# GroupNorm 2 computed in two halves of the images, and four images' edge products put behind the last spectrum product

## The chip, the core and the metric

The kernel runs on one core of a Trainium2 chip. The metric is the device time of one execution in microseconds (us). Times before the change: 1701.88, 1690.03, 1691.06, 1700.30 and 1711.91 us, median 1700.3 us. One further execution was taken with the hardware profiler; all trace times below are us from the start of its span.

Engines: PE (TensorE, matrix products), ACT (ScalarE), DVE (VectorE), POOL (GpSimd), SP (SyncE, which here only issues DMAs). Each executes its instructions in order, and an instruction that waits for a semaphore holds up all that stand behind it on that engine.

## What is computed

The input is x, 16 images of 64 channels of 128x128 pixels, float32. Two layers follow each other.

```python
# layer 0: a Hartley spectral convolution with 20x20 modes, a Gaussian blur over all 4 axes, a column mask
y = gaussian_smoothing_4d(dht_2d(modes_20x20(dht_2d(x)) mixed by w1))
x = y * mask
# layer 1
residual = x
h = group_norm(x, gn1_w, gn1_b)               # 8 groups
h = afno(h, ...)                              # 32x32 Fourier modes, two small complex layers with GELU
h = h + residual
residual = h
h = group_norm(h, gn2_w, gn2_b)               # GroupNorm 2
feats = gelu(conv1x1(h, fe_w, fe_b))
shared = mean over 2 of gelu(conv1x1(feats, shared_w[s]))
gate_w = top 4 of 16 experts, softmax, from the pixel mean of feats through small dense layers
out = shared + sum_e gate_w[e] * gelu(conv1x1(feats, expert_w[e])) + residual
```

Everything up to the second GroupNorm is linear in a few modes or acts on 32x32 modes, so the kernel stays in mode space until then. GroupNorm 2's mean and variance are also computed in mode space, and its scale and shift are folded into the weights `fsa` (one 64x64 matrix per image) and the bias `fba` of the first 1x1 convolution.

## The kernel before

The work stands in four stages of one program.

1. **Forward transform and mode mixing** (up to L367, some 265 us). The result is `ot`: 400 modes by 16 images x 64 channels.
2. **GroupNorm 1 in mode space** (L433 to L531).
3. **The spectrum loop** (`for b in range(NB)`, L630 to L659), one turn per image. Within a turn PE computes the image's 32x32 complex spectrum in two halves (L640, tiles `psx`, 32 instructions each, in two passes); the first small layer of the image before it (`layer1`, L576, with a GELU on ACT, L580); the second small layer of that image (`layer2`, L588); and `edges(b)` (L562), a product that gives the corrections at the image's borders. `layer2` ends in much work on other engines: an ACT pass with the bias (L591), two squares with accumulation for GroupNorm 2's variance (L605), on DVE a transposition (L595), copies (L599) and products with accumulation (L606), on ACT two negations (L600), and two DMAs of 512 KB that store the tile `bs` to DRAM (`bmd`, L601). `edges` ends in one DVE pass to the tile `eh` (L566) and a DMA of 130 KB to DRAM (`ehd`, L567). In turns 0 to 9 `modes(b)` runs as well (L541, L544); in turns 10 to 13 `modes_out` makes two scaled copies (L551 on ACT, L552 on DVE) and POOL issues 12 DMAs of 100 KB for each (L555). After the loop `layer2(*layer1(*first))` (L660) handles image 15.
   The tiles `xk`, `xr`, `eh`, `o1`, `o2` and `bs` have two buffers each (pool `s_w`, L627): `eh` of image b+2 can be written only when the DMA of image b has read its buffer, and the same holds for `bs`.
   A scheduler orders each engine's instructions in this stage.
4. **The pixel loop** (L975 to L989). Here the order is written out by hand (`PIECES`, L966): pieces of several images are interleaved by due times. Per image: `spectrum` (L700) loads `bm`, one single-buffered tile, in eight DMAs from DRAM (four of `bmd`, L707; four with 80-byte runs, L710) and the edge corrections (L705); `columns` (L712) transforms columns in four quarters on PE (L717), which ACT copies to the tile `u` (L721); `pixels` (L726) transforms rows in eight tiles (L737), which ACT (L748) or DVE (L750, L752) copy to the tiles `h`; `feature` (L798) does the first 1x1 convolution with `fsa` on PE (L808) and a GELU with `fba` on ACT (L812), eight per image; `gate` (L818) chooses the experts and has POOL gather their weights; `group` (L948) runs 48 convolutions per image (PE L898, GELU on ACT L903, weighted sum on DVE L907 or L913). All of this stage's PSUM comes from one pool of four double banks (`ps2`).

GroupNorm 2 is the generator `norm2` (L758). In the program before it is run once, for all 16 images, inside the pixel loop: two of its steps behind each of the first quarters of `columns` of image 0 (L985 to L987). It holds four small products on PE (L769, L775, L783, L794), some 17 short DVE instructions on 16 columns, one DVE pass that writes `fsa` for all images (L790) and one power on POOL (L786). Image 0's first `feature` needs its result.

Of the kernel before, what the change touches and what calls it, by code (L numbers as in the profile page):

```python
# [11 lines left out]
F32 = mybir.dt.float32  # L12
AF = mybir.ActivationFunctionType
ALU = mybir.AluOpType
# [4 lines left out]
NB, C, N = 16, 64, 128  # L19
# [6 lines left out]
EPS = 1e-5  # L26
# [8 lines left out]
WHOLE, SIDES = (slice(0, N),), (slice(0, N // 2), slice(N // 2, N))  # L35
BY_ACT = (0, 2, 4, 6)
CL = C // 2
NSL = 8


# [142 lines left out]
def hartley_afno_moe_kernel(ctx: ExitStack, tc: tile.TileContext, a: dict, out: bass.AP):  # L183
    nc = tc.nc
    P = 128
# [229 lines left out]
    col = lambda i, p=P: vec[0:p, i:i + 1]  # L415


    sq_pool = ExitStack()
    with tc.tile_pool(name="s_o", bufs=1) as so, \
            tc.tile_pool(name="s_p1", bufs=2, space=PSUM) as pp1, \  # L420
# [10 lines left out]
        HB, HG = NB // 2, NB // 2 * 8  # L431

        QB = NB // 4  # L433
        st = sc.tile([P, QB * C], F32, name="st")
# [148 lines left out]
        def layer2(b, o1, xr):  # L583

            ps = pp3.tile([P, 2, 512], F32, name="pso")
            for j, h in ((0, 0), (1, 1), (0, 1), (1, 0)):
                g = slice(j * C, (j + 1) * C)
                nc.tensor.matmul(ps[h * C:(h + 1) * C, j], lhsT=wx2[g, h].rearrange("p r c -> p (r c)"),  # L588
                                 rhs=o1[g, h], start=True, stop=True)
# [5 lines left out]
            nc.vector.transpose(bs[:, :, 0].rearrange("p c m -> p m c"), o2.rearrange("p (m c) -> p m c", c=MD))  # L595
            junkv, o2v, xrv = (v.rearrange("p (m c) -> p m c", c=MD) for v in (junk, o2, xr))
            for h in range(2):
                re, im = (slice(h * C + r * MD, h * C + (r + 1) * MD) for r in range(2))
                nc.vector.tensor_copy(bs[re, :, 1], bs[im, :, 0])  # L599
                nc.scalar.mul(bs[im, :, 1], bs[re, :, 0], -1.0)  # L600
                nc.sync.dma_start(bmd[b, :, h * CL:(h + 1) * CL],  # L601
                                  bs[h * C:(h + 1) * C].rearrange("p c r m -> p c (r m)"))
# [23 lines left out]

        sw = sq_pool.enter_context(tc.tile_pool(name="s_w", bufs=2))  # L627
        junk = sc.tile([P, MD * MD], F32, name="junk")
        first = second = None
        for b in range(NB):  # L630
            xk = sw.tile([P, MD * MD], F32, name="xk")
            xr = sw.tile([P, MD * MD], F32, name="xr")
            for n in range(2):
                cols = slice(n * 512, (n + 1) * 512)
                ps = pp2.tile([P, 512], F32, name="psx")
                for kc in range(4):
                    for h in range(2):
                        for ri in range(2):
                            p0 = h * C + ri * CL
                            nc.tensor.matmul(  # L640
                                ps[p0:p0 + CL], lhsT=ot[:, kc, b * C + h * CL:b * C + (h + 1) * CL],
                                rhs=spec[:, kc, ri * 1024 + n * 512:ri * 1024 + (n + 1) * 512],
                                start=(kc == 0), stop=(kc == 3))
                nc.vector.tensor_scalar(xk[:, cols], ps, gx[:, 0, b:b + 1], None, ALU.mult)
                nc.scalar.copy(xr[:, cols], ps)
                if n == 0:
                    nc.vector.tensor_scalar(xk[:, 0:1], xk[:, 0:1], gx[:, 1, b:b + 1], None, ALU.add)
                    if first:
                        second = layer1(*first)
                elif second:  # L650
                    layer2(*second)
            first = (b, xk, xr)
            edges(b)
            if b == HB:
                bn1s, bn1f, bn2s, bn2f = prepare()
            if b < K // 2:
                modes(b)
            elif b < K // 2 + QB:
                modes_out(b - K // 2)  # L659
        layer2(*layer1(*first))  # L660
        sq_pool.close()

    on_modes.close()


    with s3:
        up_, hpp, fp, gp, selp = (pool(n, q) for n, q in (
            ("u", 1), ("hp", 13), ("feats", 10), ("g", 7), ("selw", 2)))
        stgp = pool("stg", 1)
        ps2 = pool("ps2", 4, space=PSUM)  # L670


# [2 lines left out]
        def few_columns():  # L675
            return ps2.tile([P, 2, 512], F32, name="pe").rearrange("p h n -> p (h n)")[:, 0:2 * NB]
# [49 lines left out]
        def pixels(box, t):  # L726
# [31 lines left out]
        def norm2():  # L758

            w = smp.tile([P, 2, NB], F32, name="n2w")  # L760
            k = smp.tile([P, 2, NB], F32, name="n2k")
            nc.vector.tensor_tensor(w[:, 1], dcs, fold[:, P:P + 1].to_broadcast([P, NB]), ALU.mult)
            nc.vector.scalar_tensor_tensor(k[:, 0], acc[:, :, 2], 2.0, acc[:, :, 3], ALU.mult, ALU.add)
            nc.vector.scalar_tensor_tensor(k[:, 0], k[:, 0], 2.0, one_s[:, 1], ALU.mult, ALU.mult)
            nc.vector.scalar_tensor_tensor(k[:, 1], acc[:, :, 0], 2.0, k[:, 0], ALU.mult, ALU.add)
            nc.vector.scalar_tensor_tensor(w[:, 0], acc[:, :, 1], 0.5, k[:, 1], ALU.mult, ALU.add)
            yield
            z = few_columns()
            nc.tensor.matmul(z, lhsT=fold[:, 0:P], rhs=w.rearrange("p i b -> p (i b)"), start=True, stop=True)  # L769
            mh, vh = k[:, 0], k[:, 1]  # L770
            nc.vector.scalar_tensor_tensor(mh, z[:, NB:], 1.0 / N, base[:, 0], ALU.mult, ALU.add)
            nc.vector.scalar_tensor_tensor(vh, z[:, 0:NB], 1.0 / (N * N), base[:, 1], ALU.mult, ALU.add)
            yield
            z = few_columns()
            nc.tensor.matmul(z[:, 0:NB], lhsT=grp, rhs=mh, start=True, stop=True)  # L775
            m, d = w[:, 0], w[:, 1]
            nc.vector.tensor_copy(m, z[:, 0:NB])
            nc.vector.tensor_tensor(d, mh, m, ALU.subtract)
            nc.vector.tensor_tensor(d, d, d, ALU.mult)
            nc.vector.tensor_tensor(d, d, vh, ALU.add)  # L780
            yield
            z = few_columns()
            nc.tensor.matmul(z[:, 0:NB], lhsT=grp, rhs=d, start=True, stop=True)  # L783
            s, t = k[:, 0], k[:, 1]
            nc.vector.tensor_scalar(s, z[:, 0:NB], EPS, None, ALU.add)
            nc.gpsimd.tensor_tensor(s, s, mhalf[:, 0:1].to_broadcast([P, NB]), ALU.pow)  # L786
            nc.vector.tensor_scalar(s, s, col(V_GN2W), None, ALU.mult)
            nc.vector.tensor_tensor(t, m, s, ALU.mult)
            nc.vector.tensor_scalar(t, t, -1.0, col(V_GN2B), ALU.mult, ALU.add)
            nc.vector.tensor_tensor(fsa, fe2.unsqueeze(1).to_broadcast([P, NB, C]),  # L790
                                    s.unsqueeze(2).to_broadcast([P, NB, C]), ALU.mult)
            yield
            z = few_columns()
            nc.tensor.matmul(z[:, 0:NB], lhsT=few, rhs=t, start=True, stop=True)  # L794
            nc.vector.tensor_scalar(fba, z[:, 0:NB], col(V_FEB), None, ALU.add)
            yield

        def feature(box, t):  # L798
            if t == 0:
# [260 lines left out]
```

## Time and profile before

| | us |
|---|---|
| median of 5 executions (lowest, highest) | 1700.3 (1690.03, 1711.91) |
| the profiled execution, as timed | 1695.38 |
| its span, first to last instruction | 1693.6 |
| last spectrum product (L640) of image 15 ends | 502.4 |
| first quarter of `columns` of image 0 starts (L717) | 513.4 |
| its last quarter ends | 532.9 |
| first `feature` GELU of image 0 starts on ACT (L812) | 538.7 |
| its last one ends | 556.7 |
| pixel loop from then on, per image | 71 to 72 |
| mean granted TensorE clock over the span | 0.969 |

A timeline row gives the start, the duration, the engine, the source line, the operation, the output and input tiles, the shapes, a count where neighbours were merged, and in square brackets how long the engine had been idle before it and what ended that. The queue rows (SPq) give the issue of a DMA, not its landing. The windows view gives, for each stretch, the busy time of each engine, the TensorE clock granted in it as a share of full speed, the mean share of the 16 DMA engines that was busy, and GB/s. float32 products go through PE in two passes, so the counts of PE rows are twice those of the code.

### The profile page before, as it was taken

How to read it: one execution, taken by the hardware profiler on the slowest of the kernel's cores; microseconds unless marked ns; L12 is line 12 of the kernel's file. 1: busy time of each engine (PE TensorE's matmuls, PEld its weight loads, DVE VectorE, ACT ScalarE, POOL GpSimd, SP SyncE). 2: the span in 40 equal slices, each digit the busy share in tenths (PEclk: the TensorE clock that was granted, in tenths of full speed). 3: DMA queues.
4: the chain of work that ended last, by engine and by line, in shares of the span. 5: the costliest groups of instructions: out<-in, count | busy, mean ns of one | idle time of the engine just before them, and what ended most of it. 6: DMA issues, size and time to landing. Idle time of an engine off the chain costs nothing.

```text
span 1693.6 us, 61048 instructions
## 1 busy us (share of the span) xinstructions
PE 1557.7 (92%) x27144; PEld 846.3 (50%) x27144; DVE 1267.9 (75%) x1700; ACT 1272.8 (75%) x1631; POOL 150.3 (9%) x152
## 2 busy tenths in 40 slices
PE   7999958799997999999999999999999999999974
PEld 7988855233326545444444444444445445454420
DVE  0344423456663798988989889998899988999986
ACT  2233334255664898988989899998899988999975
POOL 0000011000131101101010110100101011010120
PEclk9999979899997999999999999999999999999997
DMA  9988964353574234555445555555454555545447
GB/s 385 334 311 305 309 137 122 83 129 85 129 181 108 43 46 83 90 89 92 72 81 81 100 93 74 85 82 99 89 74 85 82 100 89 75 85 81 70 72 113
DMA packets 398861, 205.02 MB, mean 121 GB/s; under 512 B 366842, under 2 KB 371942, under 8 KB 396222
## 3 DMA queue, kind: packets, MB, share of 16 engines
q1 hardware_dynamic: 394134, 193.76, 53.4%
q0 software_dynamic: 4464, 7.35, 1.8%
q8 instruction: 214, 3.51, 0.9%
q14 instruction: 49, 0.40, 0.1%
HBM read 109.86 MB, written 91.20 MB: 119 GB/s over the span
## 4 chain that ended last, share of the span: by engine, by line
PE 70%; issue 9%; DMA 9%; ACT 6%; DVE 4%; SPq 1%; POOL 1%; DVEq 0%; POOLq 0%; ACTq 0%
PE pe L898 31%; PE ps L274 8%; PE pe L717 7%; PE psx L640 6%; PE pe L737 5%; PE pe L808 5%; DMA wl<-exd,ati 5%; ACT g L903 3%; PE ps L235 3%; DMA spec_sb<-in_spec_dram 1%; PE psd L562 1%; PE psd L541 1%; DVE h L907 1%; PE pso L588 1%; PE pso L576 1%
## 5 line engine op out<-in xcount | busy, mean ns | idle before, releaser
L903 ACT ACTIVATE g<-pe,wl 128x1024 f32<-128x1024 f32 x512 | 552.3, 1201 | 49.1 <-PE pe L898 48.5
L898 PE MATMUL pe<-f,wl 64*64 64x512 f32 x4096 | 495.7, 605 | 41.5 <-DMA wl<-exd,ati 41.5
L907 DVE SCALAR_TENSOR_TENSOR h<-g,wt,h 128x1024 f32<-128x1024 f32 x384 | 472.5, 1279 | 33.9 <-ACT g L903 33.1
L907 DVE SCALAR_TENSOR_TENSOR h<-g,h 128x1024 f32<-128x1024 f32 x256 | 300.9, 1216 | 13.1 <-ACT g L903 13.1
L898 PEld LDWEIGHTS pe<-f,wl 64*64 64x64 f32 x4096 | 147.9, 135 | 267.1 <-issue 154.4
L903 ACT ACTIVATE g<-pe,vec_sb 128x1024 f32<-128x1024 f32 x256 | 269.0, 1115 | 11.5 <-PE pe L898 11.4
L898 PE MATMUL pe<-f,shw 64*64 64x512 f32 x2048 | 244.2, 595 | 0.8 <-DVE sco L850 0.4
L274 PE MATMUL ps<-fwd_sb,xt 128*64 128x64 f32 (+1 forms) x3584 | 176.2, 233 | 19.6 <-issue 13.4
L737 PEld LDWEIGHTS pe<-inv_sb,u 64*64 64x64 f32 x8192 | 155.7, 142 | 67.8 <-issue 41.8
L274 PEld LDWEIGHTS ps<-fwd_sb,xt 128*64 128x64 f32 (+1 forms) x3584 | 163.0, 147 | 24.7 <-issue 15.1
L277 ACT COPY t<-ps 128x320 f32<-128x320 f32 x128 | 53.8, 426 | 154.6 <-PE ps L274 154.4
L737 PE MATMUL pe<-inv_sb,u 64*64 64x64 f32 x8192 | 158.6, 227 | 1.9 <-ACT u L721 1.1
L913 DVE SCALAR_TENSOR_TENSOR stg<-g,wt,h 128x1024 f32<-128x1024 f32 x128 | 158.4, 1278 | 1.3 <-DMA bm<-obd 0.7
L812 ACT ACTIVATE f<-pe,fba 128x1024 f32<-128x1024 f32 x128 | 153.6, 1210 | 3.2 <-PE pe L808 3.2
L717 PEld LDWEIGHTS pe<-inv_sb,bm 116*64 116x64 f32 x4096 | 129.3, 142 | 51.9 <-ACT g L903 34.9
L717 PE MATMUL pe<-inv_sb,bm 116*64 116x64 f32 x4096 | 138.3, 228 | 2.1 <-issue 1.3
L808 PE MATMUL pe<-h,fsa 64*64 64x512 f32 x1024 | 132.5, 595 | 1.4 <-DVE h L752 1.4
L640 PE MATMUL psx<-spec_sb,ot 100*32 100x512 f32 x1024 | 117.7, 601 | 9.4 <-DMA spec_sb<-in_spec_dram 9.4
L871 POOL TENSOR_TENSOR dv<-root_e,dv 128x4 f32<-128x4 f32 x16 | 34.6, 2163 | 989.9 <-DVE ati L874 882.8
L898 PEld LDWEIGHTS pe<-f,shw 64*64 64x64 f32 x2048 | 71.4, 133 | 99.9 <-issue 69.5
L244 DVE TENSOR_TENSOR xm<-ps,pn 64x20 f32<-64x20 f32 x32 | 5.5, 171 | 152.5 <-ACT pn L240 152.3
L750 DVE COPY h<-pe 128x960 f32<-128x960 f32 x64 | 75.8, 1184 | 8.6 <-PE pe L737 8.4
(186 smaller groups left out, 1236.9 us busy)
## 6 DMA issues: line engine op xcount, KB each, us to landing
xt<-in_x_dram SPq DMA_DIRECT2D x128, 512.0 KB
out_dram<-stg SPq DMA_DIRECT2D x217, 256.0 KB
bmd<-bs SPq DMA_DIRECT2D x32, 512.0 KB
bm<-bmd SPq DMA_DIRECT2D x64, 256.0 KB
out_dram<-stg SPq DMA_DIRECT2D x31, 192.0 KB
wk<-in_w_dram SPq DMA_DIRECT2D x11, 320.0 KB
wn<-in_w_dram SPq DMA_DIRECT2D x11, 320.0 KB
spec_sb<-in_spec_dram SPq DMA_DIRECT2D x1, 3200.0 KB
```

The lines of the kernel that those rows point to most:

```text
L274: nc.tensor.matmul(ps[cols, i, :], lhsT=xt[:, i, cols], rhs=fwd1, start=True, stop=True)
L277: nc.scalar.copy(t1[:, :, c0:c0 + 8], src)
L640: nc.tensor.matmul(ps[p0:p0 + CL], lhsT=ot[:, kc, b * C + h * CL:b * C + (h + 1) * CL], rhs=spec[:, kc, ri * 1024 + n * 512:ri * 1024 + (n ...
L717: nc.tensor.matmul(ps[s * C:(s + 1) * C, i // 8, i % 8], lhsT=bm[0:KR, 16 * q + i], rhs=inv1[0:KR, s], start=True, stop=True)
L737: nc.tensor.matmul(ps[half * C:(half + 1) * C, s, j * C:(j + 1) * C], lhsT=u[rs, t * 8 + j], rhs=inv2[rs, half], start=True, stop=True)
L750: nc.vector.tensor_copy(hv[:, at:], pv[:, at:])
L808: nc.tensor.matmul(ps[p * C:(p + 1) * C, half], lhsT=fsa[rows_, box["b"]], rhs=box["h"][t][rows_, p], start=True, stop=True)
L812: nc.scalar.activation(f, ps, AF.Gelu, bias=fba[:, box["b"]:box["b"] + 1], accum_out=box["sums"][:, t:t + 1])
L898: nc.tensor.matmul(ps[half * C:(half + 1) * C, p], lhsT=w[rows_], rhs=f[rows_, half], start=True, stop=True)
L903: newest[0] = nc.scalar.activation(g, ps, AF.Gelu, bias=bias)
L907: nc.vector.scalar_tensor_tensor(h, g, share(), h, ALU.mult, ALU.add)
L913: nc.vector.scalar_tensor_tensor(box["out"][-1][:, :, c0:c0 + 16], gv, share(), hv, ALU.mult, ALU.add)
```

## The change

Four edits:

- `norm2(b0, columns_of)` now does 8 images (`HB = NB // 2`) and stands before the spectrum loop. The first half (images 0 to 7) runs inside the spectrum loop: its first step in turn 9, the next three in turn 10, the last in turn 11, with PSUM from the pool `pp1` that `edges` and `modes` use. The second half (images 8 to 15) runs in the pixel loop, one step behind every fourth `group` piece of image 0.
- `edges` of images 12 to 15 (`LATE = 4`) leaves its turns. The four run behind the loop, between `layer1` and `layer2` of image 15, with the order on PE, ACT and DVE fixed as written there.
- For image 15 the two negations (L600) go to POOL.
- The pixel loop's SBUF pools are opened in another order (`u`, `stg`, `feats`, `hp`, `g`, `selw` instead of `u`, `hp`, `feats`, `g`, `selw`, `stg`), so that `feats` and `stg`, no longer `hp` and `feats`, lie where the spectrum loop's `s_w` tiles were.

```diff
+HB = NB // 2
+LATE = 4
...
+    def norm2(b0, columns_of):
+        bs_ = slice(b0, b0 + HB)
+        w = smp.tile([P, 2, HB], F32, name="n2w")
+        k = smp.tile([P, 2, HB], F32, name="n2k")
...
+        nc.vector.tensor_tensor(fsa[:, bs_], fe2.unsqueeze(1).to_broadcast([P, HB, C]),
+                                s.unsqueeze(2).to_broadcast([P, HB, C]), ALU.mult)
...
-                nc.scalar.mul(bs[im, :, 1], bs[re, :, 0], -1.0)
+                if b == NB - 1:
+                    nc.gpsimd.tensor_scalar(bs[im, :, 1], bs[re, :, 0], -1.0, None, ALU.mult)
+                else:
+                    nc.scalar.mul(bs[im, :, 1], bs[re, :, 0], -1.0)
...
+        norms = norm2(0, lambda: pp1.tile([P, 512], F32, name="psd"))
...
-            edges(b)
+            if b < NB - LATE:
+                edges(b)
+            for _ in range({HB + 1: 1, HB + 2: 3, HB + 3: 1}.get(b, 0)):
+                next(norms)
...
-        layer2(*layer1(*first))
+        with tc.manual_schedule(engines={mybir.EngineType.PE, mybir.EngineType.Activation, mybir.EngineType.DVE}):
+            second = layer1(*first)
+            for b in range(NB - LATE, NB):
+                edges(b)
+            layer2(*second)
...
-        up_, hpp, fp, gp, selp = (pool(n, q) for n, q in (
-            ("u", 1), ("hp", 13), ("feats", 10), ("g", 7), ("selw", 2)))
-        stgp = pool("stg", 1)
+        up_, stgp, fp, hpp, gp, selp = (pool(n, q) for n, q in (
+            ("u", 1), ("stg", 1), ("feats", 10), ("hp", 13), ("g", 7), ("selw", 2)))
...
-        norms = norm2()
+        norms = norm2(HB, few_columns)
...
-                if run is columns and b == 0:
-                    next(norms, None)
+                if run is group and b == 0 and i % 4 == 3:
                     next(norms, None)
```

More of the change, by code (lines that the diff above doesn't have):

```diff
@@ L415, in hartley_afno_moe_kernel @@
     col = lambda i, p=P: vec[0:p, i:i + 1]
+    def norm2(b0, columns_of):
+        bs_ = slice(b0, b0 + HB)
+        w = smp.tile([P, 2, HB], F32, name="n2w")
+        k = smp.tile([P, 2, HB], F32, name="n2k")
+        nc.vector.tensor_tensor(w[:, 1], dcs[:, bs_], fold[:, P:P + 1].to_broadcast([P, HB]), ALU.mult)
+        nc.vector.scalar_tensor_tensor(k[:, 0], acc[:, bs_, 2], 2.0, acc[:, bs_, 3], ALU.mult, ALU.add)
+        nc.vector.scalar_tensor_tensor(k[:, 0], k[:, 0], 2.0, one_s[:, 1, bs_], ALU.mult, ALU.mult)
+        nc.vector.scalar_tensor_tensor(k[:, 1], acc[:, bs_, 0], 2.0, k[:, 0], ALU.mult, ALU.add)
+        nc.vector.scalar_tensor_tensor(w[:, 0], acc[:, bs_, 1], 0.5, k[:, 1], ALU.mult, ALU.add)
+        yield
+        z = columns_of()
+        nc.tensor.matmul(z[:, 0:2 * HB], lhsT=fold[:, 0:P], rhs=w.rearrange("p i b -> p (i b)"),
+                         start=True, stop=True)
+        mh, vh = k[:, 0], k[:, 1]
+        nc.vector.scalar_tensor_tensor(mh, z[:, HB:2 * HB], 1.0 / N, base[:, 0, bs_], ALU.mult, ALU.add)
+        nc.vector.scalar_tensor_tensor(vh, z[:, 0:HB], 1.0 / (N * N), base[:, 1, bs_], ALU.mult, ALU.add)
+        yield
+        z = columns_of()
+        nc.tensor.matmul(z[:, 0:HB], lhsT=grp, rhs=mh, start=True, stop=True)
+        m, d = w[:, 0], w[:, 1]
+        nc.vector.tensor_copy(m, z[:, 0:HB])
+        nc.vector.tensor_tensor(d, mh, m, ALU.subtract)
+        nc.vector.tensor_tensor(d, d, d, ALU.mult)
+        nc.vector.tensor_tensor(d, d, vh, ALU.add)
+        yield
+        z = columns_of()
+        nc.tensor.matmul(z[:, 0:HB], lhsT=grp, rhs=d, start=True, stop=True)
+        s, t = k[:, 0], k[:, 1]
+        nc.vector.tensor_scalar(s, z[:, 0:HB], EPS, None, ALU.add)
+        nc.gpsimd.tensor_tensor(s, s, mhalf[:, 0:1].to_broadcast([P, HB]), ALU.pow)
+        nc.vector.tensor_scalar(s, s, col(V_GN2W), None, ALU.mult)
+        nc.vector.tensor_tensor(t, m, s, ALU.mult)
+        nc.vector.tensor_scalar(t, t, -1.0, col(V_GN2B), ALU.mult, ALU.add)
+        nc.vector.tensor_tensor(fsa[:, bs_], fe2.unsqueeze(1).to_broadcast([P, HB, C]),
+                                s.unsqueeze(2).to_broadcast([P, HB, C]), ALU.mult)
+        yield
+        z = columns_of()
+        nc.tensor.matmul(z[:, 0:HB], lhsT=few, rhs=t, start=True, stop=True)
+        nc.vector.tensor_scalar(fba[:, bs_], z[:, 0:HB], col(V_FEB), None, ALU.add)
+        yield
@@ L429, in hartley_afno_moe_kernel @@
         nc.gpsimd.dma_start(exd.rearrange("e i o -> i e o"), ext)
-        HB, HG = NB // 2, NB // 2 * 8
+        HG = NB // 2 * 8
         QB = NB // 4
@@ L756, in pixels @@
             on_act(evacuate)
[L758 to L796, printed above, removed]
```

## The prediction

> **What bounds the kernel now.** I read the page's 40 slices first. PE fills nine tenths of nearly all of them; the thin places are the first slice, three at the start of the spectrum loop, and slice 13, 508 to 550 us, where PE shows 7 and its granted clock 7. That is where the spectrum loop hands over to the pixel loop, and where the change works.
>
> ```profile
> PE   7999958799997999999999999999999999999974
> PEclk9999979899997999999999999999999999999997
> DMA  9988964353574234555445555555454555545447
> ```
>
> Next the windows view (window, length, busy us of PE, PEld, DVE, ACT, POOL, then clock, DMA share, GB/s). The handover runs at clock 0.72 with the DMA engines 59% busy. Image 0's groups, the third row, have a full clock and PE busy for 70.49 of 72 us: nothing is to be won there, only lost.
>
> ```profile
> 502.00:533.00 31.00, 21.66 (x308) 16.13 (x304) 15.61 (x38) 14.67 (x22) 9.07 (x12) 0.72 0.59 162
> 533.00:557.00 24.00, 21.57 (x694) 15.59 (x696) 5.80 (x10) 15.20 (x22) 0.00 (x0) 0.86 0.29 47
> 557.00:629.00 72.00, 70.49 (x1274) 34.94 (x1268) 63.70 (x72) 68.19 (x81) 6.41 (x5) 1.00 0.24 40
> ```
>
> Then the timeline of PE through the handover. In brackets stand PE's waits: on ACT for image 15's first layer, then on GroupNorm 2 (L769 to L794). L717 takes 3.68 us a quarter at half clock, and 2.08 at full clock.
>
> ```profile
> 507.13 1.07 PE L588 MATMUL pso<-o,wx 64*64 64x512 f32 x2 [0.81 <-ACT o L580]
> 511.02 1.13 PE L588 MATMUL pso<-o,wx 64*64 64x512 f32 x6 [2.82 <-ACT o L580]
> 513.40 3.68 PE L717 MATMUL pe<-inv_sb,bm 116*64 116x64 f32 x64 [1.26 <-issue]
> 519.14 0.64 PE L769 MATMUL pe<-n2w,fold_sb 128*128 128x32 f32 x2 [2.06 <-DVE n2w L766]
> 524.92 0.58 PE L783 MATMUL pe<-n2w,grp_sb 128*128 128x16 f32 x2 [0.99 <-DVE n2w L780]
> 530.80 2.08 PE L717 MATMUL pe<-inv_sb,bm 116*64 116x64 f32 x64 [0.88 <-DVE fba L795]
> ```
>
> Last the queue of SP and the chain of waits. SP issues image 15's two stores right behind the first reload of `bm`; the first store of an earlier image took 6.71 us to land, and held DVE's transposition.
>
> ```profile
> 517.12 0.48 SPq L707 DMA_DIRECT2D bm<-bmd  x1
> 517.70 1.51 SPq L601 DMA_DIRECT2D bmd<-bs  x2
> ```
>
> ```profile
> 478.51 6.71 DMA bmd<-bs
> 485.24 2.01 DVE bs L595
> 487.27 1.06 ACT bs L600
> ```
>
> **The change part by part**, on the clock of the profiled execution (start of span = 0). Its timed 1695.4 us lies 4.9 under the median.
>
> *What it removes.* GroupNorm 2 in the handover costs PE three waits (2.06+0.99+0.88 = 3.9 us) and four products (0.64+0.61+0.58+0.40 = 2.2, 2.1 without overlap): 6.0 us between 513.4 and 532.9. Three of the four quarters also run 1.6 us slow, 4.8 together, as the clock is 0.5 from 511.9 to 529.0. If both vanished and L717 began at 513.4, image 0's features would end some 11 us earlier. This is the prize; the rest of the sum says what is paid.
>
> *First half of GroupNorm 2, turns 9 to 11.* The built program puts the fold product behind `edges(10)`, the others into turns 10 and 11. PE pays four products (2.2 us or a little less, on half the columns) and about 1 to 1.7 us waiting for DVE: 3.2 to 3.9. `edges` of 12 and 13 leave the same stretch: 2 x 1.91 = 3.8. Neither counts much: the chain pins the stretch at 485.2, the landing of image 10's late second store, from which transposition, negations and L580 lead to PE's L588 of image 13 at 490.2. The 17 short DVE instructions (0.2 us each, 3.4) and POOL's power (2.93, between its DMA issues) are ahead of that pin. Bounds -0.6 to +1.5; I take 0. Were the cover gone, it would be the same 3.2 to 3.9 less 3.8.
>
> *`edges(14)` leaves* between 492.2 and 494.2, so the last spectrum product ends at 500.5 instead of 502.4 (-1.9).
>
> *The four late edges.* PE does L588 of image 14, L576 of image 15, then four times 1.91 = 7.6 us of edges. The PSUM tile and `eh` have two buffers; the third and fourth products wait for DVE's passes over the first two (I put 1.6 us), so PE ends L588 of image 15 at about 513.3. The waits that the built program lists decide from here. `eh` of image 14 may be written only when the store of `eh` 12 has landed, and in SP's order that store stands behind both stores of image 14, the second of which waits for ACT's negation behind the copy of L551 (1.27 us). I put these stores at 507.4 and 509.7 (before: 509.3 and 510.7) and `eh` 12 at 511.4. DVE's copy L552 of turn 13 (1.49 us) now stands behind `eh` 12 and 13, so POOL, which waits for it, issues eleven stores of `modes_out` at some 509 to 515 instead of 502.8 to 510.0: beside the stores that decide. DVE executes in order, so layer 2 of image 15 on DVE, and through PSUM the first L717, stand behind `eh` 14 and 15. The landing is the unknown. By the trace's landing events an `ehd` store took 2.05 us on a quiet queue (issued 438.6), 4.6 to 6.5 in five of turns 10 to 15, and 11.5 among POOL's twelve stores (487.7); image 14's own `bmd`, which stands in front of it, took 7.7. I take 8.5, that row and a little for POOL's later stores. So `eh` 12 lands at 519.9, two DVE passes of 0.45 follow, and L717 starts at S = 521 instead of 513.4. Bounds of S: 514.5 (2.05) and 524 (11.5).
>
> *The four quarters of L717*, now back to back: 8.3 us at full clock, 14.7 at half. PE stands idle 7.7 us ahead of them, so the clock starts at 0.5; a later half-clock stretch in this trace lasted 6.8 us (535.8 to 542.65). 6.8 us at half do 3.8 us of full work, which leaves 4.5: 11 us. The last quarter ends at 532 instead of 532.9: the wait for the stores has eaten nearly all of the removed 10.8.
>
> The page "TensorE: Matmul & The Clock Gate" of the Trainium skill, section "What's actually happening", says that a window of about 3.4 us without work drops the clock to half, and a busy window of as much brings it back. By that rule the quarters would take 8.3 + 1.7 = 10 us and the sum would be 1 us lower; the 6.8 us of the trace decide. The rule speaks against the change too, since a wait of 7.7 us is long enough to lose the clock.
>
> *Image 15's stores and the new order of SBUF.* `feats` now lies on `s_w`, so image 0's first feature GELU (L812) waits until both stores of `bs` 15 (and the last `ehd`) have landed and until POOL's negations have read it. In SP's order those two stores come behind all four reloads of `bm` for image 1, each of which waits for a quarter. Before, they stood behind the first reload, issued 517.7 and landed by 524.1. From the last quarter: 0.5 issue, 0.9 for `od`, two issues of 0.75, landing 5.4 (as at 518.76): T3 + 8.5 with slack for the ring, 540.5 (T3 is the end of the last quarter). Before it was T3 + 5.8, 538.7: +1.8. POOL's two negations have no row; a POOL copy of 64x1216 took 1.2 us, and one at L427 took 1.9 (bounds 1 and 2 each). They are done by about 526, long before the stores are issued: cost 0, and if POOL were late the stores behind it would be too. The `h` tiles wait for nothing more.
>
> *Image 0's features to their end*: 18.0 us before, with half clock until 542.65. Now PE has worked for 11 us ahead of them, but L812's wait stops it again once PSUM's four tiles are full. I take 17, between the 18.0 of before and 15 for full clock (that stretch's 6.8 us at half hold 3.4 of work): the end is at 557.5 instead of 556.7 (+0.8).
>
> *Second half of GroupNorm 2 in image 0's groups.* Four products of 0.35 (half the columns) are 1.4 us of PE at least, in a window where PE idles only 1.5. DVE gets about 17 short instructions and half an `fsa` pass, 3.9 us; it has 8.3 us idle of 72, and DVE waits for POOL's power (2.93) with the weighted sums (1.2 us each) behind it: at worst 3.9+2.9 = 6.8 more. I take 2.5, bounds 1.4 and 8.2, nearer the lower end since PSUM's and `g`'s buffers hold some instructions in reserve.
>
> *Sum*: +0.8 + 2.5 = +3.3: 1698.7 against the profiled execution, 1703.6 against the median. I predict 1701, between these two. A change of 1% (17 us) is about what a measurement can tell from none, as the five runs spread over 22 us.
>
> **The rivals.**
>
> *B, faster: the stores land fast* (0.15). With `ehd` at 2.05 us S is 514.5, PE hardly loses its clock (9 us for the quarters), T3 = 523.5, the first GELU at 531 (a `bmd` landing of 4.3, as at 439.3), the features' end 16 us later at 547: -9.7+2.5 = -7.2, so 1688 on the profiled execution and 1693 on the median; 1691. For it: the 40 slices have DMA at 4 there. Against it: from 502 to 533 the windows view has 0.59, and POOL's stores are now later.
>
> *C, slower: all these stores land late* (0.20). One mechanism, DMA engines shared with POOL's stores and with the 80-byte runs of image 1's reloads: `ehd` takes 11.5 us as at 487.7, `bmd` 11.9 as at 490.9. S = 524, T3 = 535, first GELU 535+8.5+6.5 = 550, features' end 567: +10.3+2.5 = +12.8, 1708 to 1713; 1711. The turn from gain to loss is where `eh` 12 lands after about 516.6. For it: the row at 487.7 has the same neighbours. Against it: only one such row in six is that slow, and image 1's reload `od` landed in 4.0 us at 533.5.
>
> The page "DMA: Bandwidth & Descriptors", section "Issuing engines are not separate DMA queues", says that DMAs of SP and POOL end on the same 16 engines and interleave, whichever engine started them. It speaks for C; the row at 487.7 shows it once.
>
> *D, the second half binds in the groups* (0.10). DVE becomes the bound in image 0, at (63.7+3.9)/72 = 94% busy, and the whole 8.2 us is paid: +0.8+8.2 = +9.0, 1704 to 1709; 1707. Against it: it is one image of 16, with 8.3 us of DVE idle.
>
> **How the numbers follow.** The likeliest case (0.55) gives 1701; its own range is 1693 to 1709, from the 5 us between the profiled execution and the median, the second half (-1.1, +5.7) and 2 us either way for landing and clock. The range of all is 1688 (B on the profiled execution) to 1713 (the upper end of C); less than 2 in 10 is outside. Faster by over 1% is under 1683.3: only B with a low run, 0.04. Slower by over 1% is over 1717.3: only C with D on top, 0.05. Within 1%: 0.91.
>
> **What would show it.** The last L640 ends near 500.5, L588 of image 13 stays at 490. The first L717 starts near 521, and just ahead of it on DVE stands `eh` of images 14 and 15, waiting for the DMA `ehd`. The clock is 0.5 into L717 and full by its third or fourth quarter. The first L812 waits for the DMA `bmd`, near 540.5. No L769 to L794 before 557, and small gaps in front of them afterwards. It is wrong if S is under 516 (B), if L812 starts after 547 (C) or follows PE at once, or if image 0's groups take over 76 us (D).

## The result and the profile after

The changed kernel takes 1699.29 us (median of 52 runs), the kernel before, measured again beside it, 1696.21 us (94 runs). The ratio is 1.0024, 95% interval 1.0013 to 1.0034: slower by 4 us, between 2.2 and 5.8. The profiled execution spans 1699.3 us against 1693.6.

These 5.7 us cannot be read off directly. The second image's first spectrum product starts 3.58 us later in the changed kernel (325.17 instead of 321.59), and up to turn 10 the two programs keep step: taken from there, the spectrum products of images 1 to 10 start within 0.01 us of each other in the two traces. Over all profiled executions of this study that start lies between 1.5 us before and 5.8 us after 321.59. **Aligned time** below is therefore the time in a trace minus this difference of its own execution.

| aligned, us | before | predicted | after |
|---|---|---|---|
| L588 of image 13 starts | 490.2 | 490 | 490.1 |
| last spectrum product ends | 502.4 | 500.5 | 499.4 |
| columns of image 0 start (S) | 513.4 | 521 | 518.4 |
| last quarter ends (T3) | 532.9 | 532 | 528.5 |
| first feature GELU | 538.7 | 540.5 | 538.5 |
| features end | 556.6 | 557.5 | 555.9 |
| image 0's first gate product to image 1's | 65.8 | | 71.5 |
| end of the span | 1693.6 | 1696.9 | 1695.7 |

("Predicted" in the last row is 1693.6 + 3.3.) Lines of the changed kernel are numbered anew: L588 is L633, L562 L607, L566 L611, L600 L646 (POOL) and L648 (ACT), L601 L649, L717 L772, L812 L827, L825 L840, L898 L913. All times in the fences are as in the traces, not aligned. The windows view of the changed kernel, moved by 3.58 us to cover the stretches shown before:

```profile
505.58:536.58 31.00, 20.64 (x403) 16.03 (x404) 13.77 (x24) 13.90 (x20) 10.78 (x12) 0.89 0.57 141
536.58:560.58 24.00, 19.48 (x638) 13.73 (x630) 5.58 (x9) 13.15 (x20) 0.00 (x0) 0.93 0.37 70
560.58:632.58 72.00, 67.06 (x1221) 33.83 (x1224) 62.59 (x86) 64.15 (x75) 7.81 (x6) 1.00 0.22 35
```

The clock of the handover rose from 0.72 to 0.89 and from 0.86 to 0.93. Against that, PE's busy time in image 0's groups fell from 70.49 to 67.06 of 72 us: the loss lies there. From image 0's first gate product to image 1's PE is busy for 66.51 of 71.45 us, where it was busy for 64.28 of 65.79: 2.2 us more work and 3.4 us more idle time. The timeline of PE, changed kernel, shows the handover's new waits:

```profile
511.43 3.73 PE L607 MATMUL psd<-edge_sb,ot 100*64 100x260 f32 x32 [2.03 <-DVE eh L611]
515.09 1.09 PE L633 MATMUL pso<-o,wx 64*64 64x512 f32 x8
521.93 10.13 PE L772 MATMUL pe<-inv_sb,bm 116*64 116x64 f32 x256 [5.75 <-issue]
...
543.34 2.83 PE L792 MATMUL pe<-inv_sb,u 64*64 64x64 f32 x128 [2.94 <-ACT f L827]
```

The profile names no releaser for the 5.75 us ("issue"). DVE's timeline gives the likely cause: its third and fourth `eh` pass wait for DMAs, and L772 starts 0.21 us after the fourth has read its PSUM tile. The run `eh4` below tests this.

```profile
518.58 0.49 DVE L611 TENSOR_SCALAR eh<-psd,one_s 128x260 f32<-128x260 f32 x1 [5.41 <-DMA ehd<-eh]
521.23 0.49 DVE L611 TENSOR_SCALAR eh<-psd,one_s 128x260 f32<-128x260 f32 x1 [2.16 <-DMA ehd<-eh]
```

ACT's and SP's timelines show the second wait: the first GELU needs image 15's stores, and SP issues these behind all four reloads of image 1 and `od`.

```profile
542.09 1.11 ACT L827 ACTIVATE f<-pe,fba 128x1024 f32<-128x1024 f32 x1 [6.61 <-DMA bmd<-bs]
```

```profile
525.64 6.89 SPq L762 DMA_DIRECT2D bm<-bmd  x4
532.63 0.81 SPq L765 DMA_DIRECT2D bm<-od  x1
533.55 4.44 SPq L649 DMA_DIRECT2D bmd<-bs  x2
```

Last, image 0's groups in the chain of waits: POOL's power (L450) stands behind its four gathers of weights (L893). In DVE's timeline the next step (L451) waits 3.38 us for it, and DVE's later work stands behind.

```profile
580.33 2.00 POOL dv L886
582.33 0.19 issue
582.52 1.16 POOL wl L893
583.67 0.30 issue
583.98 0.98 POOL wl L893
584.96 0.30 issue
585.26 1.03 POOL wl L893
586.29 0.30 issue
586.60 0.94 POOL wl L893
587.56 1.68 POOL n2k L450
```

```profile
589.27 0.23 DVE L451 TENSOR_SCALAR n2k<-n2k,vec_sb 128x8 f32<-128x8 f32 x1 [3.38 <-POOL n2k L450]
```

### The profile page after: what moved, and what is told of

It is laid out like the page before. It is cut to its first block, busy times and chain, and to the rows that moved or that the text cites. A ratio compares the mean times of both kernels' runs of the same rounds, so it can differ in the third digit from the quotient of the medians.

```text
span 1699.3 us, 61069 instructions
## 1 busy us (share of the span) xinstructions
PE 1559.1 (92%) x27152; PEld 845.5 (50%) x27152; DVE 1270.5 (75%) x1717; ACT 1271.5 (75%) x1629; POOL 156.9 (9%) x155
## 4 chain that ended last, share of the span: by engine, by line
PE 71%; issue 9%; DMA 7%; ACT 6%; DVE 4%; POOL 1%; SPq 0%; POOLq 0%; DVEq 0%; ACTq 0%
PE pe L913 31%; PE ps L276 8%; PE pe L772 7%; PE psx L689 7%; PE pe L792 5%; PE pe L823 5%; DMA wl<-exd,ati 5%; ACT g L918 3%; PE ps L237 3%; DMA spec_sb<-in_spec_dram 1%; PE psd L607 1%; DVE h L922 1%; PE psd L586 1%; PE pso L633 1%; PE pso L621 1%
## 5 line engine op out<-in xcount | busy, mean ns | idle before, releaser
L913 PE MATMUL pe<-f,wl 64*64 64x512 f32 x4096 | 496.3, 605 | 41.6 <-DMA wl<-exd,ati 39.5
L913 PEld LDWEIGHTS pe<-f,wl 64*64 64x64 f32 x4096 | 146.8, 135 | 266.6 <-issue 140.3
L913 PE MATMUL pe<-f,shw 64*64 64x512 f32 x2048 | 244.1, 595 | 1.3 <-DVE sco L865 0.4
L827 ACT ACTIVATE f<-pe,fba 128x1024 f32<-128x1024 f32 x128 | 154.3, 1215 | 8.0 <-DMA bmd<-bs 6.6
L772 PEld LDWEIGHTS pe<-inv_sb,bm 116*64 116x64 f32 x4096 | 126.9, 140 | 56.4 <-ACT g L918 34.9
L772 PE MATMUL pe<-inv_sb,bm 116*64 116x64 f32 x4096 | 135.2, 226 | 6.8 <-issue 5.8
L886 POOL TENSOR_TENSOR dv<-root_e,dv 128x4 f32<-128x4 f32 x16 | 34.5, 2158 | 991.3 <-DVE ati L889 928.8
L913 PEld LDWEIGHTS pe<-f,shw 64*64 64x64 f32 x2048 | 71.5, 133 | 100.6 <-issue 70.5
```

Of the source, the lines that this page charges most:

```text
L772: nc.tensor.matmul(ps[s * C:(s + 1) * C, i // 8, i % 8], lhsT=bm[0:KR, 16 * q + i], rhs=inv1[0:KR, s], start=True, stop=True)
L827: nc.scalar.activation(f, ps, AF.Gelu, bias=fba[:, box["b"]:box["b"] + 1], accum_out=box["sums"][:, t:t + 1])
L913: nc.tensor.matmul(ps[half * C:(half + 1) * C, p], lhsT=w[rows_], rhs=f[rows_, half], start=True, stop=True)
```

## The experiments

The theory: the handover gains by losing GroupNorm 2, gives most of it back to two waits for stores (`ehd` ahead of the columns, `bmd` ahead of the first GELU), and image 0's groups pay for the second half. The rivals are that a part is free, or that later images absorb what a part does. "Gate distance" is the time from image 0's first gate product (L840) to image 1's.

| kernel | ratio (95%) | S | T3 | first GELU | features end | gate distance | image 1's gate to image 15's |
|---|---|---|---|---|---|---|---|
| before | 1 | 513.4 | 532.9 | 538.7 | 556.6 | 65.8 | 988.6 |
| after | 1.0024 (1.0013 to 1.0034) | 518.4 | 528.5 | 538.5 | 555.9 | 71.5 | 985.4 |
| pow_early | 1.0031 (1.0003 to 1.0059) | 518.2 | 527.5 | 537.0 | 554.5 | 74.1 | 985.5 |
| eh4 | 1.0001 (0.9974 to 1.0029) | 513.8 | 521.5 | 534.6 | 551.2 | 71.5 | 979.0 |
| bs_pool | 1.0007 (0.9985 to 1.0030) | 518.3 | 527.5 | 535.0 | 553.1 | 71.5 | 977.2 |
| late0 | 1.0036 (1.0013 to 1.0059) | 517.5 | 527.7 | 537.1 | 555.9 | 71.5 | 990.3 |
| neg_act | 1.0028 (1.0003 to 1.0052) | 518.4 | 527.6 | 532.9 | 551.3 | 71.4 | 990.4 |
| spread | 1.0002 (0.9982 to 1.0021) | 518.3 | 528.2 | 537.8 | 554.9 | 66.1 | 991.0 |
| split_only | 0.9988 (0.9965 to 1.0011) | 517.5 | 527.8 | 533.8 | 551.4 | 71.3 | 982.7 |
| edges_only | 1.0030 (1.0008 to 1.0052) | 519.0 | 540.2 | 546.8 | 564.2 | 65.9 | 987.9 |
| best_a | 1.0009 (0.9978 to 1.0040) | 515.5 | 523.1 | 532.1 | 550.3 | 66.0 | 992.3 |
| split_spread | 1.0011 (0.9981 to 1.0041) | 517.4 | 527.3 | 535.0 | 552.4 | 65.8 | 999.8 |
| old_sbuf | 1.0043 (1.0010 to 1.0077) | 518.3 | 527.5 | 540.3 | 559.8 | 71.3 | 986.8 |
| again | 1.0017 (0.9984 to 1.0051) | 518.2 | 528.1 | 538.2 | 555.5 | 71.5 | 984.1 |

The columns up to the gate distance come from one profile each, aligned; they repeat well (S is 518.2 to 518.4 in all kernels with the late edges and two buffers of `eh` but `edges_only`, the only one built on the kernel before, with 519.0). The last column is from one profile too and varies by more than most parts are worth. So each part is judged by the handover it changes, and the ratio, with 3 to 6 us on either side, is a check.

**eh4: the landing of the edge stores**

```diff
-eh = sw.tile([P, EC * 4], F32, name="eh")
+eh = seh.tile([P, EC * 4], F32, name="eh")
...
-sw = sq_pool.enter_context(tc.tile_pool(name="s_w", bufs=2))
+sw, seh = (sq_pool.enter_context(tc.tile_pool(name=n, bufs=q)) for n, q in (("s_w", 2), ("s_eh", 4)))
```

> The tile eh gets four buffers, so that the passes of images 14 and 15 no longer wait for the landing of the edge stores of images 12 and 13. Theory 1 (that landing sets the start of the first quarter of columns): the wait of PE ahead of L772, 5.75 us in the changed kernel, falls to about 1 us, the quarters take 8.3 to 9 us instead of 10.1, and the first feature GELU of image 0 starts some 6 us earlier; ratio to the kernel before 0.998 to 0.999. Theory 2 (the first feature GELU is held by image 15's stores, which stand behind image 1's reloads, and these by the DMA engines, not by the quarters): columns start earlier, but the GELU moves by less than 2 us and the ratio stays above 1.001.

The columns start 4.5 us earlier, the quarters take 7.68 us, and the features end 4.7 us earlier. The timeline of PE, `eh4`:

```profile
514.72 1.09 PE L633 MATMUL pso<-o,wx 64*64 64x512 f32 x8
517.09 7.68 PE L772 MATMUL pe<-inv_sb,bm 116*64 116x64 f32 x256 [1.28 <-ACT o L636]
530.56 1.98 PE L792 MATMUL pe<-inv_sb,u 64*64 64x64 f32 x64 [5.78 <-ACT u L776]
```

and of ACT, `eh4`:

```profile
526.75 3.76 ACT L776 COPY u<-pe 128x1024 f32<-128x1024 f32 x4 [8.35 <-DMA obd<-obk]
```

The first copy to `u` waits for a `modes_out` store of POOL; these are the stores that the change moved later, and the last of them landed at 526.53. The first GELU still waits too:

```profile
537.91 1.11 ACT L827 ACTIVATE f<-pe,fba 128x1024 f32<-128x1024 f32 x1 [4.21 <-DMA bm<-obd]
```

The row names a reload, but what landed just before 537.91 is image 15's second store (issued 531.24, landed 537.73). PE had the GELU's input ready at 536.0. So theory 1 holds for the wait ahead of the columns. The GELU gains 3.9 and not 6 us, because the copy to `u` and, last, image 15's stores hold it. The ratio, 1.0001, lies above the 0.998 to 0.999 that was expected, and its interval contains both theories' values.

**neg_act: why image 15's stores came late**

```diff
-                if b == NB - 1:
+                if b == NB:
```

No image has that number, so the branch for POOL is never taken.

> The two negations of image 15 stay on ACT; all else of the change stays. In the built program SP's order then has image 15's two stores behind the first reload of image 1, not behind all four. Theory 1 (the move of the negations to POOL is what makes these stores, and with them the first feature GELU, late): the stores land 10 us earlier, the GELU follows L823 at about 5 us behind the last quarter of columns instead of 10, the features end 4 to 5 us earlier, ratio 0.999 to 1.000. Theory 2 (ACT's 2.1 us for the negations come back in front of the u copies and eat it, or later stages absorb it): features end less than 2 us earlier, ratio 1.0015 to 1.003.

SP's timeline, `neg_act`, has the stores behind the first reload again:

```profile
521.20 0.48 SPq L762 DMA_DIRECT2D bm<-bmd  x1
521.78 1.18 SPq L649 DMA_DIRECT2D bmd<-bs  x2
523.29 5.04 SPq L762 DMA_DIRECT2D bm<-bmd  x3
```

and ACT's timeline the GELU behind PE, 5.3 us after the last quarter instead of 10.0:

```profile
532.28 1.11 ACT L827 ACTIVATE f<-pe,fba 128x1024 f32<-128x1024 f32 x1 [1.47 <-PE pe L823]
```

The features end 4.6 us earlier: theory 1, in the handover. The ratio does not show it (1.0028, theory 2's value, where theory 1 expected 0.999 to 1.000); the time from image 1's gate to image 15's was 5 us longer in this profile. So the cause of the late stores is shown, a gain of the whole kernel is not.

**bs_pool: the same stores issued by POOL**

```diff
-                nc.sync.dma_start(bmd[b, :, h * CL:(h + 1) * CL],
+                (nc.gpsimd if b == NB - 1 else nc.sync).dma_start(bmd[b, :, h * CL:(h + 1) * CL],
```

> The two stores of image 15 are issued by POOL behind its negations, no longer by SP behind image 1's reloads. Theory 1 (the first feature GELU of image 0 waits for these stores because feats lies on their tile): they are issued near 530.5 in place of 533.6 and 535.4 and land near 536.5 in place of 541.8; the GELU starts 4 to 5 us earlier, PE's idle of 2.9 us and the half clock behind it are gone, the features end 4 to 6 us earlier; ratio 0.999 to 1.001. Theory 2 (no gain: the edges' stores or the u copies hold the GELU anyway, or image 0's groups absorb it): GELU moves by under 1 us, ratio 1.002 to 1.003.

The GELU starts 3.5 us earlier and the features end 2.8 us earlier, in the direction of theory 1 and short of its 4 to 6. POOL issues the stores at 532.36 in that trace (aligned 526.6; SP's were at 530.0 aligned), but the second lands 7.5 us later, beside the reloads.

**old_sbuf: the order of the pools**

```diff
-            ("u", 1), ("stg", 1), ("feats", 10), ("hp", 13), ("g", 7), ("selw", 2)
+            ("u", 1), ("hp", 13), ("feats", 10), ("g", 7), ("selw", 2), ("stg", 1)
```

> The changed kernel with SBUF's pools in the old order, so that the tiles h, not feats, lie where the stores of image 15 read. Theory 1 (the wait for these stores moves from the first feature GELU to the first copies to h, ahead of it): the first copy to h waits for the stores until about 538.2 in aligned time, the first GELU starts near 542 instead of 538.5 and the features end 3 to 4 us later; ratio 1.004 to 1.006. Theory 2 (the new order brings nothing): features end within 1 us of the changed kernel's, ratio 1.002 to 1.003.

Theory 1: the wait moves to the first copy to `h`, and the features end 3.9 us later. ACT's timeline, `old_sbuf`:

```profile
535.54 1.01 ACT L803 COPY h<-pe 128x1024 f32<-128x1024 f32 x1 [8.39 <-DMA bmd<-bs]
```

So with the stores that late, the new order is worth 4 us.

**late0 and edges_only: the late edges, removed and alone**

```diff
-LATE = 4
+LATE = 0
```

> No late edges: the edges of images 12 to 15 go back into their turns, all else of the change stays. Theory 1 (late edges cost the handover about 5 us, through the landing of their stores, and save the loop about 3): columns of image 0 start about 1 us after the last layer of image 15, the last L689 ends 3 to 6 us later than in the changed kernel, and the end moves by -3 to +1 us; ratio 1.000 to 1.003. Theory 2 (late edges are the part that helps, since their products lie in what was PE's idle time): slower than the changed kernel by 4 us or more, ratio above 1.004.

S is 1.3 us behind the end of the last layer (516.2), but that layer itself ends 3.6 us later than in the changed kernel (512.6), as PE's turns are longer by the edges: the last spectrum product ends at 505.6, 6.2 us later, a little more than theory 1's 3 to 6. The features end where the changed kernel's do; in both the first GELU waits for image 15's stores. Where it does not wait for them, the features end alike too: 551.3 with the late edges (`neg_act`) and 551.4 without (`split_only`, which also has the old order of the pools). By the handover the late edges, beside the split, are neither cost nor gain. The ratio, 1.0036 (1.0013 to 1.0059), contains both theories' values and does not part them.

```diff
+            if b < NB - 4:
                 edges(b)
...
+            for b in range(NB - 4, NB):
+                edges(b)
+            layer2(*second)
```

> The kernel before with only the four late edges; GroupNorm 2 stays whole in the handover, negations on ACT, SBUF in the old order. Theory 1 (the late edges make the first quarter of columns wait for the landing of the edge stores, about 5 us later than before, while the loop ends 3 us earlier): the first quarter starts 4 to 6 us later in aligned time, GroupNorm 2's waits stay, ratio 1.002 to 1.005. Theory 2 (the late edges pay for themselves): ratio under 1.001.

S is 5.6 us later, as theory 1 has it, and the ratio fits. The features end 7.6 us later, more than S, for a reason that was not foreseen: the clock stays at half. The timeline of PE, `edges_only`, whose columns are L722 and GroupNorm 2's products L774 to L799:

```profile
519.42 3.68 PE L722 MATMUL pe<-inv_sb,bm 116*64 116x64 f32 x64 [4.11 <-issue]
525.27 0.64 PE L774 MATMUL pe<-n2w,fold_sb 128*128 128x32 f32 x2 [2.17 <-DVE n2w L771]
525.84 3.68 PE L722 MATMUL pe<-inv_sb,bm 116*64 116x64 f32 x64
...
531.56 3.68 PE L722 MATMUL pe<-inv_sb,bm 116*64 116x64 f32 x64
...
536.94 3.68 PE L722 MATMUL pe<-inv_sb,bm 116*64 116x64 f32 x64 [0.67 <-DVE fba L800]
```

**split_only: GroupNorm 2's split alone**

The edits are those of `late0`, `neg_act` and `old_sbuf` together; what is left of the change is the split (and the written-out order behind the loop).

> Only GroupNorm 2 is split: edges in their turns, negations on ACT, SBUF in the old order. Theory 1 (the split takes 6 us and part of the 4.8 us of half clock out of the handover, and pays 3.5 us in turns 9 to 11 that the loop no longer hides, and 3 to 5.7 us in image 0): the last quarter of columns ends some 4 to 6 us earlier than in the kernel before, in the aligned time, and the end lies within 3 us of it; ratio 0.998 to 1.002. Theory 2 (the split is free in the loop and in image 0, so the gain of 8 us or more shows): ratio 0.995 to 0.996.

T3 comes 5.1 us earlier and the features end 5.3 us earlier, although the last spectrum product is 3.2 us later: theory 1. The gate distance is 71.3, so 5.5 us are paid again in image 0.

**pow_early, spread and split_spread: the second half elsewhere**

```diff
-                if run is group and b == 0 and i % 4 == 3:
+                if run is group and b == 0 and i % 2 == 1:
```

> The five steps of the second half of GroupNorm 2 come behind every second group piece of image 0 instead of every fourth, so POOL's power is issued ahead of the four gathers of weights. Theory 1 (DVE's 3.4 us wait for the power behind the gathers is what makes image 0's groups 5.7 us longer): the wait shrinks to about 1.7 us, the time between the first and second gate products falls by 2 to 4 us against the changed kernel's 71.45 us, and the ratio to the kernel before falls from 1.0024 to about 1.001. Theory 2 (the cost is the four products and the 17 short DVE instructions themselves, wherever they stand): the time between the gates stays within 1 us of 71.45 and the ratio stays at 1.002 to 1.003.

Theory 1 falls in this form. DVE's wait for the power shrank to 1.87 us, as foreseen, but the gate distance grew to 74.1. The answer on PE's waits, `pow_early`, from gate to gate:

```profile
PE pe L913 <- DMA wl<-exd,ati: 2.0, 1, 2.0
PE pe L913 <- DVE sco L865: 1.9, 1, 1.9
```

The steps now stand ahead of the gate's own DVE instructions. POOL's first instruction for the selection (L886) starts 23.3 us after the gate's first product instead of 20.1 in the changed kernel and 17.9 before, the gathered weights are late, and two half-clock stretches of 3.4 us fall into the image. So the wait for the power alone does not explain the 5.7 us; which of the steps around the gate costs what stays open.

In `spread` and `split_spread` the same line is another:

```diff
-                if run is group and b == 0 and i % 4 == 3:
+                if run is group and 1 <= b <= 5 and i == 31:
```

> The five steps of the second half run in images 1 to 5, one behind the 32nd group piece of each, instead of all five in image 0; they are needed by image 8. Theory 1 (the second half costs 5.7 us in image 0, because its chain of short DVE instructions and POOL's power stand around the gate and the gathers): the time from the first to the second gate product falls from 71.5 to 66 us, as before the change, and each of the five images pays at most 1 us; ratio 0.999 to 1.001. Theory 2 (image 0's loss is given back by image 3 anyway, as the distance of the changed kernel from the one before shrinks from 4.9 to about 2 us there): the ratio stays within 0.001 of 1.0024.

The gate distance is 66.1, as before the change: it is the second half's steps that made image 0 longer. But the way from image 1's gate to image 15's is 991.0 us, 5.6 more than the changed kernel's. The ratio, 1.0002 (0.9982 to 1.0021), has theory 1's value, and its interval reaches into theory 2's.

> As the kernel with only the split (no late edges, negations on ACT, old SBUF order), with the second half's steps spread over images 1 to 5. Theory 1 (the split alone is the part worth having, and image 0 was its cost): the features of image 0 end near 551 in aligned time, the gates of images 0 and 1 are 66 us apart, ratio 0.996 to 0.998. Theory 2 (spread steps cost as much as they save, a little in each of five images): ratio within 0.001 of 0.9988.

The gate distance fell to 65.8, and the way behind it grew to 999.8, by 17 us; the ratio is not below that of `split_only`. Theory 2, if anything.

Part of that growth is the steps themselves. From image 1's gate to image 6's, where they now run, `spread` and `best_a` take 358.3 and 359.0 us with 13.7 us of half clock in that stretch. `late0`, `edges_only` and `pow_early`, which run no step there, have as much half clock and take 353.4 to 354.9. `split_spread` takes 362.9 with 17.1 us of half clock, the kernel before 358.5 with as much. So the five images pay between 3.4 and 5.6 us together for the 5.4 that image 0 saves.

**best_a: the three repairs together**

The edits are those of `eh4`, `neg_act` and `spread`.

> Three repairs together: eh with four buffers, image 15's negations back on ACT, the second half's steps spread over images 1 to 5. Theory 1 (the three losses are independent: the landing of the edge stores, the late stores of image 15, and the second half in image 0): in aligned time columns start near 513.8, the features of image 0 end near 546, that is 10 us before the kernel before, the distance of the first two gates is 66 us; the five spread steps cost up to 3 us later; ratio 0.994 to 0.997. Theory 2 (half-clock stretches in later images, whose number differs from execution to execution, swallow what the handover gains): the features end as said, but the ratio stays above 0.998.

The columns start at 515.5, not 513.8. The features end 6.3 us earlier than before the change, not 10: the first copy to `u` starts only after the quarters are nearly done, just behind the landing of POOL's last `modes_out` store (525.24 and 525.09 in the trace), and the GELU then follows PE. The gate distance is 66.0. The ratio is 1.0009 (0.9978 to 1.0040): theory 2's number. Half-clock stretches are only a part of its reason, as the five steps cost time of their own. No version of this study is shown to beat the kernel before; `split_only` comes nearest with 0.9988 (0.9965 to 1.0011).

**again: the changed kernel once more**

No edit.

> The changed kernel once more. Theory 1 (the number of half-clock stretches in images 1 to 15 differs between executions of one program, and makes most of the spread of the runs): the handover repeats to within 1 us in aligned time, but the time from the second to the last gate differs from 985.4 us by 3 us or more, and with it the total of half-clock time by 5 us or more. Theory 2 (that time belongs to the program): both repeat to within 2 us. Ratio 1.001 to 1.0035 in either case.

The handover repeats within 0.5 us. Theory 1 half fails: the way from image 1's gate to image 15's differs by 1.3 us only, not by 3 or more, while the half-clock time after 640 us differs by 8.1 us (62.8 against 54.7). Which images are long does change: from gate to gate the third image (image 2) takes 69.3 us in one profile of this program and 71.1 in the other, image 7 71.2 and 68.8. The windows view of two such stretches, `again` (the first opens and closes 1.6 us ahead of image 2's and image 3's gates, the second is image 7):

```profile
698.99:769.99 71.00, 68.67 (x1234) 34.55 (x1230) 64.29 (x73) 65.94 (x77) 6.33 (x5) 0.98 0.53 86
1052.47:1121.23 68.76, 67.15 (x1233) 33.47 (x1229) 64.21 (x72) 65.70 (x77) 6.34 (x5) 1.00 0.54 89
```

The same work in both, and 2.2 us more where the clock is 0.98: 1.5 us of it PE's busy time, the rest idle. Whether a kernel like `split_spread`, with 999.8 us, has more such images by its own doing, or by chance in its one profile, stays open.

## Why the prediction was right

The change in time agrees (+3.3 us predicted, about +4 measured, 2.2 to 5.8), and so does the mechanism: gains in the handover, given back to stores and to image 0. The 1701 lay between the sums on two starting points, the profiled execution and a median of five; the 94 runs put the start at 1696.21.

The sum agrees in part by luck, as two terms missed in opposite directions. The handover was put at +0.8 and measured -0.8, the second half at +2.5 and measured +5.7. To image 1's gate that makes +4.9 instead of +3.3. The +2.1 at the end of the span comes out near because the later images took 3.2 us less than in the one profile of the kernel before, and such differences are not shown to belong to the program. The terms named for the likeliest case's own range, on the two starting points, add up to 1695.6 to 1711.3, not to its 1693 to 1709; the measured time lies in both. Step by step:

- **First half of GroupNorm 2: net 0, right; its reason, wrong.** L633 of image 13 starts at 490.1. But "the chain pins the stretch at 485.2" was not what held it: in `late0`, which keeps the first half and puts the edges back, that instruction starts at 493.9. The pin covered only the 0.4 us that PE idled there. It is the fallback of the prediction that holds, 3.2 to 3.9 us paid with 3.8 us of removed edges: `late0` pays 3.7, and in the changed kernel itself image 12's spectrum products start 3.7 us later than before, ahead of the places where the edges left.
- **Loop's end**: 499.4 instead of 500.5, on the good side: L588 of image 13 had taken 2.15 us and takes 1.09 now.
- **The landing of `ehd`: the mechanism right, the size too long.** 8.5 us was taken; the stores of images 12 and 13 took 5.1 and 7.1 (issued 513.38 and 514.01, landed 518.45 and 521.11 in the changed kernel's trace), and it was the second that counted. S came 2.6 us earlier than predicted.
- **Four quarters**: 11 us predicted, 10.13 measured; 9.2 to 10.4 in the other kernels that run them back to back with half clock in them, 7.68 in `eh4` at full clock. The 8.3 taken for full clock was 0.6 too much. The clock was 0.5 from 520.5 for 6.8 us, as long as the prediction took.
  By the Trainium skill, "TensorE: Matmul & The Clock Gate", section "What's actually happening", the prediction had estimated 10 us. That is nearer, but not by the page's count: the stretch lasted two windows of 3.4 us and not one. Nor did the clock fall only after a whole window without work, as the last section shows.
- **First GELU**: it waits for `bmd` as predicted, 10.0 us behind T3 instead of 8.5, as SP took 2.56 us to issue the second store and that landed in 6.4 instead of 5.4. POOL's two negations took 5.94 us together, some 3 each, outside their bounds of 1 to 2; they still ended at 530.1, ahead of the issue at 533.55. That they cost nothing was wrong in another way: moving them is what put the stores behind four reloads (`neg_act`, 4.6 us). The prediction saw that order in the built program and did not ask which edit made it.
- **Features**: 17.4 us, 17 predicted.
- **Second half: mis-sized.** 2.5 us taken, bounds 1.4 to 8.2; image 0's gate distance grew by 5.7 us, 2.2 of them PE's work and 3.4 its idle time. The reserve of buffers that the prediction counted on did not cover the steps. DVE's wait behind the gathers is one place where it ran out, but `pow_early` shows that it is not the whole cause, and the rest stays open.

Rival C put the turn from gain to loss at `eh` 12 landing after 516.6. That store landed at 514.9 aligned, but the one of image 13, which counted, at 517.5; the handover still ended 0.8 us ahead, and the loss came from image 0. Rival B is excluded by S. Rival D's place was right and its size between: the gate distance says 5.7 of its 8.2 us, and DVE was not the bound, with 62.59 of 72 us busy.

## What to carry to other kernels

Before work is moved to just ahead of a stage, look for the DMA that the stage's buffers wait for: here two stores of 130 KB decided the start of the stage, and two more buffers moved it by 4.5 us. When a scheduler orders a queue, a small edit on one engine can move another engine's DMAs; compare the built orders edit by edit, not only for the whole change. Work that is "hidden" behind a busy engine has to be placed against the chains of short instructions there, and work that is needed late should be tested at several places, since its cost here moved for the greater part from image 0 to others rather than vanish.

## What the runs showed of the hardware

- Apart from the last of each span, half-clock stretches came in lengths of 3.4, 6.8, 10.2, 13.7, 17.1 and 30.7 us, one to nine times 3.41. The longest, in `edges_only` from 517.3, went on though PE was busy for 21.79 of 30.70 us:

```profile
517.30:548.00 30.70, 21.79 (x380) 19.45 (x383) 9.34 (x28) 9.16 (x12) 3.43 (x2) 0.50 0.48 112
```

  It began within a wait of 4.1 us (515.3 to 519.4); PE's later gaps in it were 0.4 to 2.2 us long.
- Waits well under 3.4 us can precede half clock. In `pow_early` single waits of 1.91 and 1.99 us in image 0 were each followed by a half-clock stretch of 3.41 us; in the 3.4 us just ahead of the two stretches PE was busy for 1.67 and 1.41 us.
- A negation of 32x1024 float32 took 2.93 us on POOL (mean of 2.76 and 3.10) and 1.05 on ACT. The power took 2.93 us on 128x16 and 1.68 on 128x8, so half the columns took 57% of the time.
- Two executions of one program put their half-clock stretches into different images; the two images shown differ by 2.2 us. Up to turn 1, where the work of all kernels is the same, the profiled executions differ by up to 7.3 us (-1.5 to +5.8).
